# Fewer sum products, last numerators by four heads, and five smaller edits in a four-stage transformer kernel

## The chip, the cores and the metric

The kernel runs on one core of one Trainium2 chip. A core has five engines that run beside each other[...]: PE (TensorE, matrix products), DVE (VectorE), ACT (ScalarE), POOL (GpSimd) and SP (SyncE, which here only issues transfers). Each engine works through its own queue of instructions in order. The metric is the device time of one execution in microseconds (us), the median of several runs.

## The reference, cut to what matters

The input x has four sequences (b) of 512 tokens with 512 features; each sequence has a memory of 1024 rows. Four residual blocks follow each other; each normalises x (layer norm), computes something, and adds it to x, times the tanh of a learned gate.

```python
x = x + tanh(g_xattn[0]) * attention_1_head(layernorm(x), memory, mask)   # stage a
x = x + tanh(g_ffn[0])   * ternary_experts(layernorm(x))                  # stage b
x = x + tanh(g_xattn[1]) * attention_16_heads(layernorm(x), memory)       # stage c
x = x + tanh(g_ffn[1])   * experts_gelu(layernorm(x))                     # stage d

# stage c, for each head (head size 32)
scores = Q @ K.T / sqrt(32)
ctx = softmax(scores) @ V            # numerators exp(score - max), divided by their sum
out = ctx @ Wo.T + bo

# stage d, for expert e, which has tokens 64*e to 64*e+63 of every sequence
h = gelu(xe @ w1[e] + b1[e])
y = h @ w2[e] + b2[e]
```

In stage b the tokens are quantised before the expert's product: a row of a token is scaled, rounded to whole numbers and clipped at 127.

## The kernel before, in words

**Stage a** (to about 300 us) goes through 16 tiles of 128 tokens. Its loop over n runs from -2: `prepare` normalises a tile on DVE, `turn_x` transposes it on PE, `scores` multiplies it with the memory, `softmax` adds a bias that carries the mask (L455) and takes exponentials on ACT, `turn_p` and `readout` make the weighted memory, `finish` adds it to x. Ahead of the loop, ACT takes the tanh of the four gates (L615) and loads the table for logarithm and exponential (L616); then come `prepare(0)`, `set_mask(0)` (the mask's bias, L366, on DVE) and `set_valid(0)` (a reduce over the mask and a product with the gate, L372 and L374). Four weight loads are issued from ACT's queue after the first `turn_x`. Beside the attention the loop prepares stage b: `route_1` to `route_4` normalise, quantise and route the tokens. L531 scales a row and rounds it by adding a large number; L532 takes that number off again, clips, and writes bf16, both on DVE. The same loop makes ternary weights of stage b (`weight_load`, `weight_sum`, `weight_scale`, `weight_store`).

**Stage b** (to about 430 us) runs the ternary experts on sorted tokens. The change does not touch it.

**Stage c** (to about 1284 us) has an order written out by hand: for PE, ACT, DVE and POOL the instructions stand in the order of the program text. The 16 heads of 4 sequences make NG = 16 groups of four heads. A group has U = 16 steps, each one half (two heads, p) of one of the 8 memory chunks (c) of 128 rows. The loop over t runs through all 256 steps. In one turn of it:

- `score_pairs(t)` makes two score tiles for the maxima of step t + 21 (c_s, L1096; DVE takes the row maxima, L1117) and two numerator tiles for step t: a product with ones that puts the negative maximum into the bank (c_t, L1103), the transposed scores on top (L1108), and the exponential on ACT (L1115) into a tile c_e of two heads.
- `add_chunks(t)` sums numerators over chunks, 128x1024 at a time, into four accumulators c_acc: two halves of the chunks (c from 0 to 3, c from 4 to 7) for each pair of heads p. POOL does it, except for the odd steps of the last group, which DVE does two turns later.
- `weigh` multiplies numerators of step t - 4 with the values (c_o, L1147).
- `sum_chunks`, 8 steps after each half of a group, sums an accumulator over its 128 rows with products with ones (c_sum, L1179, four products); for the first half ACT copies the result to c_rec (L1187), for the second DVE adds it (L1189). `divide` then takes reciprocals (L1193) and multiplies (L1196).

All tiles of this stage but c_o come from one ring of 7 PSUM banks (`ps_s`), in the order in which they are asked for: score tiles, numerator tiles, sums, projections and transposes. `project_q`, `project_k`, `project_v` and `project_out` stand at certain steps between. From t = T0 = 236 on no scores are left to make. There the first three sequences are already normalised and transposed for stage d: `normal_d` on DVE (L1216), `turn_d` on PE (d_tp, L1224), `leave_d` on DVE or ACT in turns, one tile a step, twelve in all.

**Stage d** has no hand-written order; a scheduler places its instructions. For each of 8 experts: 16 blocks of the first product (d_h, L1457) with GELU on ACT (L1463), then for two halves of 128 tokens the second product (d_o, L1473, 16 products of 512 columns), to which DVE adds the bias b2 in PSUM (L1477), and then the update of x with the gate for each of the two sequences in the half (L1480). After every second expert a tile of x is complete and is stored (L1487). b2 comes by a load from POOL's queue into one of two buffers (L1450).

Of the kernel before, what the change touches and what calls it, by code (L numbers as in the profile page):

```python
# [18 lines left out]
P = 128  # L19
# [8 lines left out]
def flamingo_kernel(  # L28
# [131 lines left out]
    def ln_stats(b, tag, eng):  # L160

        mv = mv_of.pop(b)
        return mv[:, :, 0], rsqrt(mv[:, :, 1], NT, f"{tag}_{b}", eng)
# [137 lines left out]
    with ExitStack() as st:  # L301
# [61 lines left out]
        def set_mask(p):  # L363
            mk8 = mem_of[p][2]
            bias = wk.tile([P, M], FP, tag="mbias", name=f"mbias_{p}")
            nc.vector.tensor_scalar(bias, mk8, -1.0, -NEG / scale0, ALU.add, ALU.mult)  # L366
            mem_of[p][3] = bias

        def set_valid(p):
# [147 lines left out]
        def route_2(n):  # L517
            xn, am = route_of[n]
            tp = ps_1.tile([P, NK, P], FP, tag="tpx", name=f"b_tp_{n}")
            for k in range(NK):  # L520
                nc.tensor.transpose(tp[:, k, :], xn[:, bass.ts(k, P)], ident)
            xnT = wk.tile([P, NK, P], FP, tag="bxnT", name=f"b_xnT_{n}", bufs=1)
            nc.scalar.copy(xnT, tp)
            amc = sst.tile([P, 1], FP, tag="amc", name=f"b_amc_{n}")
            nc.vector.tensor_scalar(amc, am, Q_EPS, None, ALU.max)  # L525
            ra = sst.tile([P, 1], FP, tag="ra", name=f"b_ra_{n}")
            nc.vector.reciprocal(ra, amc)
            sx = sst.tile([P, 1], FP, tag="sx", name=f"b_sx_{n}")
            nc.vector.tensor_scalar(sx, ra, 127.0, None, ALU.mult)
            row = wk.tile([P, RW], U8, tag="row", name=f"b_row_{n}", bufs=3)  # L530
            nc.vector.tensor_scalar(xn, xn, sx, MAGIC, ALU.mult, ALU.add)  # L531
            nc.vector.tensor_scalar(  # L532
                row[:, 0 : 2 * D].bitcast(BF), xn, -MAGIC, 127.0, ALU.add, ALU.min
            )
            rx = sst.tile([P, 1], FP, tag="rx", name=f"b_rx_{n}")
            nc.gpsimd.tensor_scalar(rx, amc, 1.0 / 127.0, None, ALU.mult)  # L536
            nc.gpsimd.tensor_scalar(
                row[:, 2 * D : RW].bitcast(FP), rx, rx, rx, ALU.mult, ALU.mult
            )
            route_of[n] = xnT, row  # L540
# [71 lines left out]
                weight_sum(q + 2)  # L612

        load_first()
        nc.scalar.activation(gates, graw, AF.Tanh)  # L615
        nc.scalar.preload_act_table_set("natural_log_exp_and_others")  # L616
        prepare(0)
        set_mask(0)
        set_valid(0)
        h = 0  # L620
        for n in range(-2, NQ):
            if 0 <= n < NQ:
                turn_p(n)
            if n >= 0:
                some_weights(h)
                h += 1
            if 0 <= n - 1 < NQ:
                route_1(n - 1)
            if 0 <= n + 1 < NQ:
                scores(n + 1)  # L630
            if n + 2 < NQ:
                turn_x(n + 2)
            if n == -2:
                for q in range(4):
                    weight_load(q, nc.scalar)
            if 0 <= n + 1 < NQ:
                softmax(n + 1)
            if n + 3 < NQ:
                prepare(n + 3)
            if n >= 0 and n % 4 != 3:  # L640
                some_weights(h)
                h += 1
            if n == NQ - 1:
                break
            if 0 <= n - 2 < NQ:
                route_3(n - 2)
            if 0 <= n < NQ:
                finish(n, readout(n))
            if 0 <= n - 1 < NQ:
                route_2(n - 1)  # L650
            if 0 <= n - 2 < NQ:
                route_4(n - 2)
            if n >= -1 and (n + 5) % NT == 0 and n + 5 < NQ:
                load_x((n + 5) // NT)
                load_memT((n + 5) // NT)
                load_mem((n + 5) // NT)
            if n >= 0 and (n + 4) % NT == 0 and n + 4 < NQ:
                set_mask((n + 4) // NT)
            if n >= 0 and (n + 3) % NT == 0 and n + 3 < NQ:
                set_valid((n + 3) // NT)  # L660
# [292 lines left out]
    with ExitStack() as st:  # L953
# [11 lines left out]
        U = 16  # L965
        AHEAD = 21
        LAG = 4

        ones_bf = big.tile([P, P], BF, tag="ones_bf", name="c_ones_bf")
        nc.gpsimd.memset(ones_bf, 1.0)  # L970
# [104 lines left out]
        def score_pairs(t):  # L1075

            todo_t = todo_s = ()
            if t >= 0 and t < NG * U:
                g, k = divmod(t, U)
                c, p = divmod(k, 2)  # L1080
                todo_t = (2 * p, 2 * p + 1)
            u = t + AHEAD
            if u < NG * U:
                gs, ks = divmod(u, U)
# [21 lines left out]
            for i in todo_t:  # L1106
# [2 lines left out]
                    t_of[i], lhsT=kT_of[g][r, bass.ts(c, P)], rhs=qT_of[g][r, :],  # L1109
                    start=False, stop=True,  # L1110
                )
            if todo_t:
                e_of[t] = big.tile([P, 2, S], FP, tag="e", name=f"c_e_{t}", bufs=EB)
            for i in todo_t:
                nc.scalar.activation(e_of[t][:, i % 2, :], t_of[i], AF.Exp)  # L1115
            for i in todo_s:
                nc.vector.tensor_reduce(  # L1117
                    mxn_of[gs][:, j, i, n : n + 1], s_of[i], AX.X, ALU.max
# [41 lines left out]
        def add_chunks(t):  # L1160
# [11 lines left out]
            else:  # L1172
                acc = acc_of[g, c // 4, p]
                eng.tensor_tensor(acc, acc, e_of[t], ALU.add)  # L1174

        def sum_chunks(g, h):
            ps = ps_s.tile([P, S], FP, tag="s", name=f"c_sum_{g}_{h}")
            for i in range(4):
                nc.tensor.matmul(  # L1179
                    ps[i * HD : (i + 1) * HD, :], lhsT=ones[:, 0:HD],  # L1180
                    rhs=acc_of[g, h, i // 2][:, i % 2, :], start=True, stop=True,
                )
            if h == 1 and g == NG - 1:
                return ps
            if h == 0:
                rec_of[g] = wk.tile([P, S], FP, tag="rec", name=f"c_rec_{g}", bufs=1)
                nc.scalar.copy(rec_of[g], ps)  # L1187
            else:
                nc.vector.tensor_tensor(rec_of[g], rec_of[g], ps, ALU.add)  # L1189

        def divide(g, q):
            rq = rec_of[g][:, bass.ts(q, P)]
# [5 lines left out]


        out_of, tp_of = {}, {}  # L1200
        T0 = NG * U - AHEAD + 1

        def reuse_memory():

# [104 lines left out]
        for t in range(-LEAD, NG * U + LAG):  # L1309
# [9 lines left out]
            if (t + LEAD) % U == 0 and 0 <= t + LEAD < NG * U:  # L1319
# [3 lines left out]
                if g >= NK:  # L1323
                    project_k(g, 0)
                    project_k(g, 1)
            d = t - T0
            if 2 <= d < 14:
                leave_d(
                    tp_of.pop(d - 2), *divmod(d - 2, NT), (nc.vector, nc.scalar)[d % 2]
# [1 line left out]
            if 0 <= d < 12:  # L1331
                b, j = divmod(d, NT)
                mean, rstd = stats_of[b]
                xn_of[b, j] = normal_d(b, j, mean[:, j : j + 1], rstd[:, j : j + 1])
            if t >= -AHEAD:
                score_pairs(t)
            if t in early:
                f, args, h = early[t]
# [3 lines left out]
            for b, w, d in [(1, 4, t + LEAD)] + [(b, 8, t + 84 - b * NK * U) for b in (2, 3)]:  # L1342
                if 0 <= d < 4 * w and d % w == 0:
                    back = wk.tile([P, D], FP, tag="xn", name=f"b_back_{b}_{d}")
                    fetch_row(back, b, d // w)
                if 0 <= d < 4 * w and d % w == w // 2 + 1:
                    add_row(b, d // w, nc.gpsimd)
                if w < d < 5 * w and d % w == 1:
                    ln_part(b, d // w - 1, "c")
                if d == 4 * w + 3:  # L1350
                    stats_of[b] = ln_stats(b, "c", nc.gpsimd)
            if 0 <= t < NG * U and not last_odd(t):
                add_chunks(t)
            if last_odd(t - 2):
# [5 lines left out]
            if 0 <= t - LAG < NG * U:  # L1360
                g, k = divmod(t - LAG, U)
                if k == 0 and g % NK == 0 and g:
                    for c in range(NM):
                        project_v(g // NK, c)
                weigh(g, k // 2, k % 2)
            d = t - T0 - 1
            if 0 <= d < 12:
                b, j = divmod(d, NT)
                tp_of[d] = turn_d(ps_s, "s", b, j, xn_of.pop((b, j)), None)
            d = t - 2 * LAG  # L1370
            if 0 <= d < NG * U - 1 and d % 8 == 7:
                sum_chunks(d // U, d % U // 8)

            if (t + LEAD) % (NK * U) == (NK - 1) * U and 0 <= t:
# [43 lines left out]
    with ExitStack() as st:  # L1418
# [13 lines left out]
        for e in range(E):  # L1432
# [33 lines left out]

            r0 = (e * CAP) % P
            j = (e * CAP) // P
            for half in range(B * CAP // P):
                ps = ps_o.tile([P, D], FP, tag="o", name=f"d_o_{e}_{half}")  # L1470
                for f in range(NF):
                    n, fo = divmod(f, NF // NW)
                    nc.tensor.matmul(  # L1473
                        ps, lhsT=hT[:, f, bass.ts(half, P)], rhs=w2c[n][:, fo, :],
                        start=(f == 0), stop=(f == NF - 1),
                    )
                nc.vector.tensor_tensor(ps, ps, b2_t, ALU.add)  # L1477
                for i in range(P // CAP):
                    b = half * (P // CAP) + i
                    nc.vector.scalar_tensor_tensor(  # L1480
                        xs[b][r0 : r0 + CAP, j, :], ps[i * CAP : (i + 1) * CAP, :],
                        gate_f1[r0 : r0 + CAP, :],
                        xs[b][r0 : r0 + CAP, j, :], ALU.mult, ALU.add,
                    )
                    if r0 + CAP == P:
                        eng = nc.sync if e == E - 1 else nc.gpsimd
                        eng.dma_start(out=out[b, bass.ts(j, P), :], in_=xs[b][:, j, :])  # L1487


# [43 lines left out]
```

## Time and profile before

| what | value |
|---|---|
| median of 3 runs | 1734.85 us (1733.16 to 1736.13) |
| the profiled execution itself | 1734.78 us |
| its span, first to last instruction | 1733.0 us |
| mean granted TensorE clock | 0.999 |
| HBM traffic over the span | 99 GB/s |

The rows of the profile name a line of the kernel, an engine, an operation and its tiles as out<-in, with the number of partitions and elements. These carry the places that the change touches (busy time in us, mean of one in ns):

| row | count | busy | mean |
|---|---|---|---|
| DVE L1117, maxima of c_s | 512 | 325.2 | 679 |
| POOL L1174 and L1171, additions to c_acc | 186 | 436.8 | 2374 |
| ACT L1115, exponentials c_e | 512 | 277.9 | 594 |
| PE L1179, c_sum (two passes a product) | 256 | 33.4 | 593 |
| DVE L1193, reciprocals of c_rec | 60 | 56.3 | 941 |
| DVE L1189, additions to c_rec | 15 | 10.3 | 687 |
| DVE L1216, twelve d_xn in stage c | 12 | 17.1 | 1435 |
| DVE L532, whole-number rows | 16 | 6.9 | 428 |
| DVE L1477, additions of b2 | 16 | 11.2 | 700 |

An fp32 product appears on PE as two passes, each with its weight load. Ends of products are modelled, so PE reads as busy even where a product waits for a bank; what a step really takes is seen in the distance from one start of a line to the next.

### The profile page before, as it was taken

The numbers are of one execution on the slowest core, as the hardware profiler recorded it, in microseconds if no ns is written. First come the engines' busy times: TensorE is split into PE (matmuls) and PEld (weight loads), VectorE is DVE, ScalarE is ACT, GpSimd is POOL, SyncE is SP. The second block draws the span as 40 slices with busy tenths as digits, with TensorE's granted clock in tenths as the row PEclk, the third lists the DMA queues.
The fourth block names the chain that finished last, engine by engine and source line by source line (L and its number), as shares of the span: only waits on it lengthen the run. The fifth ranks groups of instructions, "written<-read, shape, count | busy, mean of one in ns | idle before, by whom it ended". The sixth has DMA issues, their size and how long they took to land.

```text
span 1733.0 us, 22272 instructions
## 1 busy us (share of the span) xinstructions
PE 1676.3 (97%) x8805; PEld 826.0 (48%) x8805; DVE 846.4 (49%) x1758; ACT 655.1 (38%) x1155; POOL 635.7 (37%) x594
## 2 busy tenths in 40 slices
PE   5999999888999999999999999999999999999998
PEld 3554555344433434334343343433356776667764
DVE  3888886565577562665626656166850001100111
ACT  3655663485046352353523535235530111011110
POOL 1011111563269494474945748357630000000000
PEclk9999999999999999999999999999999999999999
DMA  9366532595010000010000100001036364534530
GB/s 347 138 245 228 185 128 103 168 325 168 25 50 2 7 13 7 1 50 7 13 7 1 50 1 1 1 1 50 1 120 233 131 220 152 183 139 152 201 121 25
DMA packets 76072, 173.12 MB, mean 100 GB/s; under 512 B 4480, under 2 KB 5008, under 8 KB 75968
## 3 DMA queue, kind: packets, MB, share of 16 engines
q1 hardware_dynamic: 61888, 128.07, 21.0%
q0 software_dynamic: 8368, 33.02, 5.8%
q10 hardware_dynamic: 5712, 10.62, 1.6%
q8 instruction: 69, 1.13, 0.3%
q14 instruction: 35, 0.29, 0.1%
HBM read 153.06 MB, written 18.62 MB: 99 GB/s over the span
## 4 chain that ended last, share of the span: by engine, by line
PE 81%; DVE 9%; POOL 3%; ACT 2%; DMA 2%; issue 2%; DVEq 0%; ACTq 0%; POOLq 0%
PE d_h L1457 13%; PE d_o L1473 13%; PE c_t L1108 9%; PE c_s L1096 8%; PE c_o L1147 8%; PE c_vp L1052 6%; PE c_k L1035 5%; PE c_q L1013 3%; PE a_s L444 3%; PE a_o L479 3%; PE c_out L1065 2%; PE c_t L1103 2%; PE c_sum L1179 2%; DMA b_wt<-tern_d,widx 1%; DVE w_all L412 1%
## 5 line engine op out<-in xcount | busy, mean ns | idle before, releaser
L1117 DVE TENSOR_REDUCE c_mxn<-c_s 128x1 f32<-128x512 f32 x512 | 325.2, 679 | 258.0 <-PE c_s L1096 258.0
L1115 ACT ACTIVATE c_e<-c_t 128x512 f32<-128x512 f32 x512 | 277.9, 594 | 246.2 <-PE c_t L1108 232.9
L1174 POOL TENSOR_TENSOR c_acc<-c_acc,c_e 128x1024 f32<-128x1024 f32 x124 | 291.3, 2378 | 104.7 <-ACT c_e L1115 104.6
L1108 PE MATMUL c_t<-c_qT,c_kT 32*128 32x512 f32 x1024 | 283.7, 595 | 0.0
L1096 PE MATMUL c_s<-c_kT,c_qT 32*128 32x512 f32 x1024 | 276.2, 639 | 0.0
L1473 PE MATMUL d_o<-d_w,d_hT 128*128 128x512 f32 x512 | 221.0, 592 | 0.0
L1457 PE MATMUL d_h<-d_xnT,d_w 128*128 128x256 f32 x992 | 215.4, 379 | 0.0
L1477 DVE TENSOR_TENSOR d_o<-d_o,d_b 128x512 f32<-128x512 f32 x16 | 11.2, 700 | 404.6 <-PE d_o L1473 404.6
L1171 POOL TENSOR_TENSOR c_acc<-c_e,c_e 128x1024 f32<-128x1024 f32 x62 | 145.5, 2367 | 165.8 <-ACT c_e L1115 165.8
L1457 PEld LDWEIGHTS d_h<-d_xnT,d_w 128*128 128x128 f32 x992 | 188.5, 190 | 28.6 <-issue 3.3
L1463 ACT ACTIVATE d_hT<-d_h,b_t 128x256 f32<-128x256 f32 x128 | 60.7, 474 | 350.0 <-PE d_h L1457 350.0
L1147 PE MATMUL c_o<-c_e,c_v 128*32 128x256 f32 x2048 | 162.9, 391 | 0.0
L1473 PEld LDWEIGHTS d_o<-d_w,d_hT 128*128 128x128 f32 x512 | 97.3, 190 | 119.0 <-issue 118.6
L1096 PEld LDWEIGHTS c_s<-c_kT,c_qT 32*128 32x128 f32 x1024 | 74.3, 183 | 116.7 <-issue 41.0
L1147 PEld LDWEIGHTS c_o<-c_e,c_v 128*32 128x32 f32 x2048 | 40.7, 108 | 182.4 <-issue 171.2
L1103 PE MATMUL c_t<-c_mT,c_ones_bf 3*128 3x512 bf16 x512 | 126.9, 380 | 0.0
L444 PE MATMUL a_s<-memT,a_xnT 128*128 128x512 f32 x256 | 117.0, 611 | 0.7 <-ACT a_xnT L436 0.7
L479 PE MATMUL a_o<-mem,a_prT 128*128 128x512 f32 x256 | 114.6, 598 | 0.2 <-ACT a_prT L472 0.2
L1108 PEld LDWEIGHTS c_t<-c_qT,c_kT 32*128 32x128 f32 x1024 | 100.7, 185 | 6.2 <-issue 3.9
L536 POOL TENSOR_SCALAR b_rx<-b_amc 128x1 f32<-128x1 f32 x16 | 3.5, 221 | 244.6 <-DVE b_amc L525 244.6
L1035 PE MATMUL c_k<-c_memT,w_all 128*128 128x512 f32 x192 | 85.3, 597 | 0.0
L1052 PE MATMUL c_vp<-w_all,c_memT 128*128 128x512 f32 x192 | 83.2, 594 | 0.0
(288 smaller groups left out, 1874.5 us busy)
## 6 DMA issues: line engine op xcount, KB each, us to landing
d_w<-in_w SPq DMA_DIRECT2D x63, 1024.0 KB, 5.6
w_all<-in_wuT SPq DMA_DIRECT2D x7, 1024.0 KB, 6.1
w_all<-in_wdT SPq DMA_DIRECT2D x7, 1024.0 KB, 6.0
memT<-in_memT SPq DMA_DIRECT2D x3, 2048.0 KB, 14.6
mem<-in_mem SPq DMA_DIRECT2D x3, 2048.0 KB, 11.2
tern_d<-t ACTq DMA_DIRECT2D x24, 256.0 KB, 4.3
w_all<-in_wgT SPq DMA_DIRECT2D x6, 1024.0 KB, 6.3
c_memT<-in_memT SPq DMA_DIRECT2D x3, 2048.0 KB, 8.1
```

The costliest lines, as they stand in the source:

```text
L444: nc.tensor.matmul(s_ps[:, bass.ts(h, HALF)], lhsT=xnT[:, k, :], rhs=memT_t[:, k, bass.ts(h, HALF)], start=(k == 0), stop=(k == NK - 1),)
L479: nc.tensor.matmul(o_ps, lhsT=prT[:, c, :], rhs=mem_t[:, c, :], start=(c == 0), stop=(c == NM - 1),)
L1035: nc.tensor.matmul(ps, lhsT=wk_t[:, k, bass.ts(o, P)], rhs=memT_of[b][:, k, bass.ts(n, HALF)], start=(k == 0), stop=(k == NK - 1),)
L1052: nc.tensor.matmul(ps, lhsT=memT_of[b][:, k, bass.ts(c, P)], rhs=wv_t[:, k, :], start=(k == 0), stop=(k == NK - 1),)
L1096: nc.tensor.matmul(s_of[i], lhsT=qT_of[gs][r, bass.ts(j, P)], rhs=kT_of[gs][r, bass.ts(n, HALF)], start=True, stop=True,)
L1108: nc.tensor.matmul(t_of[i], lhsT=kT_of[g][r, bass.ts(c, P)], rhs=qT_of[g][r, :], start=False, stop=True,)
L1115: nc.scalar.activation(e_of[t][:, i % 2, :], t_of[i], AF.Exp)
L1117: nc.vector.tensor_reduce(mxn_of[gs][:, j, i, n : n + 1], s_of[i], AX.X, ALU.max)
L1147: nc.tensor.matmul(o_bank[i * HD : (i + 1) * HD, hs], lhsT=v_all[:, c, bass.ts(o * 4 + i, HD)], rhs=e_of[g * U + 2 * c + i // 2][:, i % 2, ...
L1174: eng.tensor_tensor(acc, acc, e_of[t], ALU.add)
L1457: nc.tensor.matmul(ps[:, 0 : B * CAP], lhsT=w1c[n][:, k, bass.ts(fo, P)], rhs=xnT[:, k, :, bass.ts(e, CAP)], start=(k == 0), stop=(k == NK ...
L1473: nc.tensor.matmul(ps, lhsT=hT[:, f, bass.ts(half, P)], rhs=w2c[n][:, fo, :], start=(f == 0), stop=(f == NF - 1),)
```

## The change

1. **Sums of stage c.** For groups 0 to 14 the two accumulator halves are first added by DVE (`join_chunks`, 128x1024, at steps 16g + 18 and 16g + 19, one for each pair of heads), and `sum_chunks` runs once a group, on the joined half. ACT copies the result to c_rec; DVE's addition is gone. The last group keeps its two sums.
2. **Last numerators.** From T0 = 236 on `score_pairs` runs at even steps only and makes the numerators of four heads, those of steps t and t + 1; `weigh` does both halves at even steps.
3. **Turns for stage d** begin at R0 = 223 instead of T0 = 236.
4. **Bias of stage d.** b2 is multiplied by the gate and added to x in SBUF, once an expert (one multiplication of 128x512 and four additions of 64x512), instead of twice into PSUM. Nothing in it depends on the products, and the scheduler puts these instructions of all eight experts ahead of the first update of x; those of the first expert stand between DVE's work on the last tiles of the last sequence.
5. **Last product.** The second half of the last expert is computed in two halves of 256 columns, each with its own updates and stores.
6. **Start.** The tanh of the gates, with a table load on each side of it, moves behind the first tile's root and behind ACT's four weight loads; `set_valid(0)` moves to n = -1, which puts it on DVE between the normalisation of tile 1 and the softmax of tile 0.
7. **To GpSimd:** the mask's bias (`set_mask`) and L532, the whole-number rows.

```diff
         def set_mask(p):
...
-            nc.vector.tensor_scalar(bias, mk8, -1.0, -NEG / scale0, ALU.add, ALU.mult)
+            nc.gpsimd.tensor_scalar(bias, mk8, -1.0, -NEG / scale0, ALU.add, ALU.mult)
...
-            nc.vector.tensor_scalar(
+            nc.gpsimd.tensor_scalar(
                 row[:, 0 : 2 * D].bitcast(BF), xn, -MAGIC, 127.0, ALU.add, ALU.min
             )
...
         load_first()
-        nc.scalar.activation(gates, graw, AF.Tanh)
         nc.scalar.preload_act_table_set("natural_log_exp_and_others")
         prepare(0)
         set_mask(0)
-        set_valid(0)
...
             if n == -2:
                 for q in range(4):
                     weight_load(q, nc.scalar)
+                nc.scalar.activation(gates, graw, AF.Tanh)
+                nc.scalar.preload_act_table_set("natural_log_exp_and_others")
+            if n == -1:
+                set_valid(0)
...
+        T0 = NG * U - AHEAD + 1
...
-                todo_t = (2 * p, 2 * p + 1)
+                todo_t = (2 * p, 2 * p + 1) if t < T0 else range(4)
...
-            if todo_t:
-                e_of[t] = big.tile([P, 2, S], FP, tag="e", name=f"c_e_{t}", bufs=EB)
-            for i in todo_t:
-                nc.scalar.activation(e_of[t][:, i % 2, :], t_of[i], AF.Exp)
+            for m, i in enumerate(todo_t):
+                if m % 2 == 0:
+                    e_of[t + m // 2] = e_t = big.tile(
+                        [P, 2, S], FP, tag="e", name=f"c_e_{t + m // 2}", bufs=EB
+                    )
+                nc.scalar.activation(e_t[:, i % 2, :], t_of[i], AF.Exp)
...
+        def join_chunks(g, p):
+            acc = acc_of[g, 1, p]
+            nc.vector.tensor_tensor(acc, acc, acc_of[g, 0, p], ALU.add)
+
         def sum_chunks(g, h):
...
-            if h == 0:
-                rec_of[g] = wk.tile([P, S], FP, tag="rec", name=f"c_rec_{g}", bufs=1)
-                nc.scalar.copy(rec_of[g], ps)
-            else:
-                nc.vector.tensor_tensor(rec_of[g], rec_of[g], ps, ALU.add)
+            rec_of[g] = wk.tile([P, S], FP, tag="rec", name=f"c_rec_{g}", bufs=1)
+            nc.scalar.copy(rec_of[g], ps)
...
-        T0 = NG * U - AHEAD + 1
+        R0 = NG * U - 33
...
-            d = t - T0
+            d = t - R0
...
-            if t >= -AHEAD:
+            if t >= -AHEAD and (t < T0 or t % 2 == 0):
                 score_pairs(t)
...
+            d = t - U - 2
+            if d >= 0 and d % U < 2 and d // U < NG - 1:
+                join_chunks(d // U, d % U)
             if 0 <= t < NG * U and not last_odd(t):
                 add_chunks(t)
...
-                weigh(g, k // 2, k % 2)
-            d = t - T0 - 1
+                if t < T0:
+                    weigh(g, k // 2, k % 2)
+                elif t % 2 == 0:
+                    weigh(g, k // 2, 0)
+                    weigh(g, k // 2, 1)
+            d = t - R0 - 1
...
-            if 0 <= d < NG * U - 1 and d % 8 == 7:
+            if 0 <= d < NG * U - 1 and d % 8 == 7 and (d % U == 7) == (d // U == NG - 1):
                 sum_chunks(d // U, d % U // 8)
...
+                last = e == E - 1 and half == B * CAP // P - 1
+                for o in ((slice(0, D // 2), slice(D // 2, D)) if last else (slice(0, D),)):
...
-                nc.vector.tensor_tensor(ps, ps, b2_t, ALU.add)
+                    if half == 0:
+                        nc.vector.tensor_scalar(b2_t, b2_t, gate_f1, None, ALU.mult)
+                        for b in range(B):
+                            xt = xs[b][rows, j, :]
+                            nc.vector.tensor_tensor(xt, xt, b2_t[rows, :], ALU.add)
```

## What is predicted, before the changed kernel ran

> **What bounds the kernel now.** I read the page's busy shares, the chain that ended last, and then the timeline of each stage that the change touches.
>
> ```profile
> PE 1676.3 (97%) x8805; PEld 826.0 (48%) x8805; DVE 846.4 (49%) x1758; ACT 655.1 (38%) x1155; POOL 635.7 (37%) x594
> PE 81%; DVE 9%; POOL 3%; ACT 2%; DMA 2%; issue 2%; DVEq 0%; ACTq 0%; POOLq 0%
> ```
>
> PE carries the chain; DVE and POOL are half idle on average. An average hides that in the 16-head stage PE and DVE run in step. Four steps of its timeline (start, duration, engine, line):
>
> ```profile
> 1200.35 0.70 PE L1096 MATMUL c_s<-c_kT,c_qT 32*128 32x512 f32 x2
> 1201.50 1.29 DVE L1117 TENSOR_REDUCE c_mxn<-c_s 128x1 f32<-128x512 f32 x2 [0.47 <-PE c_s L1096]
> 1202.21 0.70 PE L1096 MATMUL c_s<-c_kT,c_qT 32*128 32x512 f32 x2
> 1202.87 2.35 POOL L1171 TENSOR_TENSOR c_acc<-c_e,c_e 128x1024 f32<-128x1024 f32 x1 [0.42 <-ACT c_e L1115]
> 1203.37 1.29 DVE L1117 TENSOR_REDUCE c_mxn<-c_s 128x1 f32<-128x512 f32 x2 [0.58 <-PE c_s L1096]
> ```
>
> A plain step lasts 1.76 or 1.87 us, mean 1.82; DVE's two maxima take 1.29. They begin 1.16 after the step's first product and leave DVE 0.52 free. Seven PSUM banks serve four tiles a step, so the second numerator of step t+1 takes the bank that the first maximum of step t frees. What happens when DVE gets more than 0.52 is seen where reciprocals (L1193, 0.94 each) stand between the maxima: c_s begins at 630.57, 632.33, 634.20, 636.21, 638.20, 640.29, so steps of 1.87 become 2.00 to 2.09. PE's lost time is the delay of the maxima less about 0.13.
>
> The second thing to see is DVE adding while POOL adds:
>
> ```profile
> 1242.06 2.64 POOL L1174 TENSOR_TENSOR c_acc<-c_acc,c_e 128x1024 f32<-128x1024 f32 x1 [2.38 <-ACT c_e L1115]
> 1242.40 3.38 DVE L1171 TENSOR_TENSOR c_acc<-c_e,c_e 128x1024 f32<-128x1024 f32 x1
> 1246.73 2.36 POOL L1174 TENSOR_TENSOR c_acc<-c_acc,c_e 128x1024 f32<-128x1024 f32 x1 [2.03 <-ACT c_e L1115]
> 1249.30 1.21 DVE L1174 TENSOR_TENSOR c_acc<-c_acc,c_e 128x1024 f32<-128x1024 f32 x1
> ```
>
> Alone, DVE's add takes 1.21. Begun while POOL adds, it ends 1.08 after POOL's end (1244.70 to 1245.78). All four such pairs in the trace do so (the others begin at 1258.20, 1261.63 and 1265.13).
>
> **Part 1, sums of the 16-head stage.** Removed: 15 groups of c_sum products, 1.04 us of PE each (steps with one last 2.62 to 2.85 instead of 1.76 or 1.87). DVE's rec add (0.69) goes too, but the steps after it show no delay now, so that is worth 0; ACT's copy moves to an ACT gap (0.7 a step). Added: 30 joins, DVE adds of 128x1024, after the maxima of steps 16g+18 and 16g+19. POOL's first add of the next group overwrites what join 0 reads, so it waits for join 0, and then runs ahead of join 1.
>
> One group, in us from the start of step 16g+18. Maxima end at 2.4; join 0 runs 2.4 to 3.5; POOL's add 3.6 to 5.9; the next maxima 3.5 to 4.7; join 1 waits to 5.9 and ends at 7.0; the maxima of 16g+20 then begin at 7.0, not 3.63 + 1.16 = 4.8. PE loses 2.2 - 0.13 = 2.1. This needs POOL's last add of the old group to be over at 2.4. By the trace it ends at about 0 for groups 4, 8, 12; at 2.0 for 0; at 2.7 for 1, 5, 9, 10, 11; at 4.0 for 2, 3, 6, 7. The last three classes come about 1.0 later, since POOL's queue stays and PE skips the sum before. So: 2.1 x 3; 2.6 for group 0; for the 2.7 class join 0 ends at 4.8, join 1 at 8.3, a loss of 3.3 (group 10); 1, 5, 9 already stall 0.5 there: 2.8 x 3; group 11 hides join 1 behind the value projection (27.7 us of PE): 1.7; in 2 and 6 join 0 ends at 6.1, POOL's row add (1.26) runs beside the maxima and join 1 ends at 8.4: 3.4 x 2; 3 and 7 hide join 1 like group 11, but the maxima behind join 0 begin at 6.0 instead of 2.9: 2.95 x 2. Sum 6.3 + 2.6 + 3.3 + 8.4 + 1.7 + 6.8 + 5.9 = **+35**, against **-13** for the sums of groups 0 to 12 (13 and 14 come below).
>
> [...] By the shortest row (1.2) two joins exceed two gaps by 2 x (1.09 - 0.52) - 0.13 = 1.0 a group: break-even with the sum. [...] Ends for the pair of numbers: 0 and +45.
>
> **Part 2, turns of the last stage begun at step 223.** Steps 223 to 235 last 25.8 now (1193.7 to 1219.5). Twelve d_tp turns (4 transposes, 0.585 of PE each) move in: +7.0; one sum goes: -1.0. DVE gets 12 normalisations (0.55 alone, mean 1.44 now, the rest waiting for POOL) and six copies (0.68) ahead of maxima, in a gap of 1.1 (step 2.4). In some 8 steps POOL is adding: 1.44 + 0.34 - 1.1 = 0.7 each, 5.6; in 3 steps a reciprocal: 0.94 + 0.55 + 0.34 - 1.1 = 0.7 each, 2.1; group 13's joins 2.2. Together **+16**; without waits +7.
>
> **Part 3, numerators by four heads from step 236.** From 1219.5 to the last sum (1270.0) 50.5 us pass now. PE would need 10 pairs of 2.4 (1.82 and a second weigh of 0.57) and two sums, 26. POOL is next: 10 adds of 2.36 after step 236, the rest of one before (2.8), maxima split (1.9), two oT (2.6), two bias adds ahead of the last add (2.4): 33.3, and 7 DVE adds that exclude it, 1.09 each: 41. So **-9.6**. Ends: -20 if POOL overlaps, 0 if the late joins hold the sum product of group 14 for long. Parts 2 and 3 together +6.
>
> **Part 4, the bias of the last experts.** In the built order DVE's first product of b2 with the gate stands before the reciprocal root, d_xn and d_xnT of the last tiles. It waits for b2's load:
>
> ```profile
> 1284.29 1.20 POOL L1450 DMA_DIRECT2D d_b<-in_b  x2 [11.86 <-PE c_out L1254]
> 1286.77 0.54 DVE L1216 TENSOR_SCALAR d_xn<-x,mv_e,rstd_e 128x512 f32<-128x512 f32 x1
> 1287.36 0.66 PE L1224 MATMUL d_tp<-ident,d_xn 128*128 128x128 f32 x4
> ...
> d_b<-in_b POOLq DMA_DIRECT2D x1, 256.0 KB, 7.0
> ```
>
> Issued at 1284.3, 7.0 to land: 1291.3. With 0.55 for the product and 0.87 for root and d_xn the turn begins at 1292.7 instead of 1287.36; the next turn stands behind two 64x512 adds, a copy and d_xn, 2.7 us, of which PE fills 2.1. **+6.0** (4 to 7). The other seven loads come in pairs behind it, within some 40 us; the first expert result is wanted at 1327.9 and two banks cover the rest: 0.
>
> **Part 5, the end.** Now after the last product: b2 add 0.70, two updates 0.75 each, store. The add goes (-0.70), the updates halve (-0.75), the store of half size has about 0.2 less to move: **-1.6**. The halved product pays nothing by the row: L1457's 992 passes of 256 columns take 215.4 us, 0.217 each, half of L1473's 221.0/512 = 0.432, with a 0.19 weight load in each. [...]
>
> **Part 6, the start and the first stage.** The first root waits for the tanh's gates:
>
> ```profile
> 9.60 1.28 ACT L615 ACT_TABLE_LOAD   x1 [9.60 <-DMA graw<-in_g_ffn]
> 12.41 0.29 ACT L280 ACTIVATE lv_a<-mv_a,eps_t 128x1 f32<-128x1 f32 x1
> ...
> 26.06 1.22 DVE L455 CUSTOM_DVE_ANT_0 a_pr<-a_s,mbias 128x1024 f32<-128x1024 f32 x1 [1.60 <-PE a_s L444]
> ```
>
> Its input is there at 6.73, so it comes 5.7 earlier. But ACT now has four weight loads ahead of the tanh, and the fourth is issued 6.6 after the first (15.54, 22.18): then to about 16.9; two table loads, tanh and root bring tile 1 normalised to 21.9, the validity reduce (1.37, now before the softmax) to 23.3 against 26.06: **-2.8** (0 to -5.7). Whole-number rows: DVE sheds 16 x 0.43 and the masks 3 x 0.68; POOL's op of that shape is near its copy (0.60) or its add (1.27), and DVE's next two-input add waits for it: **0** (-5 to +6).
>
> **Sum.** 1734.8 - 2.8 - 13 + 35 + 16 - 9.6 + 6 - 1.6 = 1764.8; taken as 1764. The base is the profiled execution's own 1734.78 (span 1733.0), equal to the median of 1734.85.
>
> **Rivals.** (a) Joins cost DVE's own time alone: part 1 is 0, part 2 some +13: 1740. For it: POOL's adds might fall elsewhere; against: the written dependence puts one between the joins. 15%. (b) The other side: the banks take up DVE's lag, and joins and normalisations stall nothing: -2.8 - 13 + 6.0 - 9.6 + 6 - 1.6 = 1720. It decides if a delay of the maxima under one step is free; the reciprocal steps, lengthened by a delay of 0.3, say no. 9%. (c) Each join loses to one more POOL add in half the groups (2.36 x 13/2) and the first stage pays 6: 1786. 10%. The forecast: 66%. That the change does not do what it says is out: the built order has the 60 products fewer.
>
> **Range and chances.** 1743 to 1780 leaves (b), (c) and half of (a) out. About 0.2%, 3.5 us, is what this kernel's measurement tells from no change. Faster: (b) and a little of (a), 10%. Same: 4%. Slower: 86%.
>
> **What would show it.** Steps 16g+20 and 16g+21 lasting together 2 to 3 us more, DVE's joins near 2 us in the mean, c_sum halved; PE idle 5 us at the second d_tp of the last stage, behind DVE waiting for d_b; the softmax of tile 0 near 23. Joins at 1.2 with steps of 1.9 would break part 1.

## The result and the profile after

The changed kernel takes **1814.68 us** (median of 4 runs, 1812.37 to 1815.5) against 1735.49 for the kernel before in the same session: ratio 1.0453, interval 1.0432 to 1.0473. It is slower, as forecast, but by 79 us where 29 were forecast, and outside the range. Its profiled execution took 1814.32 (span 1812.5).

Three rows of the page after: PE's busy time, the granted TensorE clock in 40 slices, and the chain that ended last.

```profile
PE 1716.9 (95%) x8717; PEld 845.0 (47%) x8717; DVE 923.6 (51%) x1779; ACT 655.2 (36%) x1156; POOL 686.4 (38%) x614
PEclk9999999999998999999899999999989999999999
PE 65%; DVE 7%; POOL 6%; issue 2%; DMA 2%; ACT 1%; DVEq 0%; ACTq 0%; POOLq 0%
```

88 matmuls fewer are recorded, yet PE is busy 41 us longer: the same products took longer. The clock row says how. Before, it is 9 (at least 90%) in every slice; after, three slices show 8. The mean granted clock fell from 0.999 to 0.970. Span times lost clock is 1812.5 x 0.030 = 54 us, against 2 before. DVE and POOL took 13% of the chain instead of 12%; the chain does not name the clock.

The place is seen best at one pair of joins. The timeline of the changed kernel in group 2 (start, duration, engine, line; lines between are left out at ...):

```profile
614.11 9.29 POOL L1179 TENSOR_TENSOR c_acc<-c_acc,c_e 128x1024 f32<-128x1024 f32 x4
...
619.71 1.29 DVE L1122 TENSOR_REDUCE c_mxn<-c_s 128x1 f32<-128x512 f32 x2 [0.58 <-PE c_s L1099]
...
621.12 4.58 DVE L1183 TENSOR_TENSOR c_acc<-c_acc 128x1024 f32<-128x1024 f32 x1
...
623.36 1.25 POOL L248 TENSOR_TENSOR x<-x,b_back 128x512 f32<-128x512 f32 x1
625.62 1.28 DVE L1122 TENSOR_REDUCE c_mxn<-c_s 128x1 f32<-128x512 f32 x2
625.84 2.34 POOL L1176 TENSOR_TENSOR c_acc<-c_e,c_e 128x1024 f32<-128x1024 f32 x1 [1.23 <-DVE c_acc L1183]
626.35 0.58 PE L1106 MATMUL c_t<-c_mT,c_ones_bf 3*128 3x512 bf16 x1 [3.04 <-DVE c_mxn L1122]
...
626.35 2.28 PE L1111 MATMUL c_t<-c_qT,c_kT 32*128 32x512 f32 x4
626.82 2.44 DVE L1183 TENSOR_TENSOR c_acc<-c_acc 128x1024 f32<-128x1024 f32 x1
```

Join 0 (at 621.12) stands behind the last of POOL's four adds (to 623.40) and its row add (to 624.61) and lasts 4.58; a join during which POOL does not add lasts 1.21 to 1.22. The profile shows no wait ahead of it: the two engines meet here in the adds themselves, not by a semaphore alone. The maxima behind it free the bank late, and PE idles for 3.04. This is the mechanism of the forecast. Then the four numerator products take 2.28; in group 0, at whole clock, the same four take 1.23. The windows of this stretch (length, busy time of each engine with the number of its instructions, granted clock PEclk):

```profile
core 0: us, PE busy (x) PEld busy (x) DVE busy (x) ACT busy (x) POOL busy (x), PEclk, DMA share, GB/s
619.45:622.87 3.42, 3.42 (x35) 1.16 (x32) 3.04 (x3) 2.28 (x5) 3.42 (x2) 1.00 0.00 0
622.87:626.28 3.41, 0.44 (x4) 0.00 (x0) 3.41 (x3) 0.36 (x1) 2.18 (x3) 1.00 0.00 0
626.28:629.69 3.41, 3.34 (x16) 1.03 (x16) 3.41 (x4) 1.09 (x2) 2.19 (x2) 0.50 0.00 0
629.69:633.11 3.42, 3.42 (x18) 1.13 (x17) 2.19 (x5) 1.03 (x2) 3.25 (x3) 0.50 0.00 0
```

The window with the stall still has the whole clock. The two windows **behind** it, in which PE is busy again, run at half: 34 matmuls where the window ahead of the stall did 35 in one. So the stall of 3.0 is followed by a loss of another 3.4. All half stretches of the trace last 3.41, 6.83 or 10.24 us, but for the one that the end of the span cuts, and all start on one grid of 3.413 us (from 411.24 to 1366.97 are 280 steps). Ten of the thirteen pairs of joins of groups 0 to 12 have such a stretch behind them, 68.3 us in all.

### The profile page after: what moved, and what is told of

The parts are those of the page before. It is cut to its first block, busy times and chain, and to the rows that moved or that the text cites. A ratio compares the mean times of both kernels' runs of the same rounds, so it can differ in the third digit from the quotient of the medians.

```text
span 1812.5 us, 22176 instructions
## 1 busy us (share of the span) xinstructions
PE 1716.9 (95%) x8717; PEld 845.0 (47%) x8717; DVE 923.6 (51%) x1779; ACT 655.2 (36%) x1156; POOL 686.4 (38%) x614
## 4 chain that ended last, share of the span: by engine, by line
PE 65%; DVE 7%; POOL 6%; issue 2%; DMA 2%; ACT 1%; DVEq 0%; ACTq 0%; POOLq 0%
PE d_o L1489 12%; PE d_h L1470 12%; PE c_t L1111 7%; PE c_s L1099 6%; PE c_vp L1055 6%; PE c_k L1038 5%; PE c_o L1152 5%; PE c_q L1016 3%; DVE c_acc L1183 3%; POOL c_acc L1179 2%; PE c_out L1068 2%; POOL c_acc L1176 2%; DVE c_mxn L1122 2%; DMA b_wt<-tern_d,widx 1%; PE c_t L1106 1%
## 5 line engine op out<-in xcount | busy, mean ns | idle before, releaser
L1111 PE MATMUL c_t<-c_qT,c_kT 32*128 32x512 f32 x1024 | 295.0, 633 | 0.0
L1099 PE MATMUL c_s<-c_kT,c_qT 32*128 32x512 f32 x1024 | 292.0, 671 | 0.0
L1489 PE MATMUL d_o<-d_w,d_hT 128*128 128x512 f32 (+1 forms) x544 | 221.4, 567 | 1.1 <-DVE x L1501 1.1
L1501 DVE SCALAR_TENSOR_TENSOR x<-d_o,gates,x 64x512 f32<-64x512 f32 (+1 forms) x34 | 24.4, 718 | 385.2 <-PE d_o L1489 384.8
L1152 PE MATMUL c_o<-c_e,c_v 128*32 128x256 f32 x2048 | 168.5, 406 | 0.5 <-ACT c_ou L1160 0.5
L1489 PEld LDWEIGHTS d_o<-d_w,d_hT 128*128 128x128 f32 x544 | 103.3, 190 | 114.9 <-issue 109.8
L1106 PE MATMUL c_t<-c_mT,c_ones_bf 3*128 3x512 bf16 x512 | 134.4, 396 | 21.7 <-DVE c_mxn L1122 21.3
L1099 PEld LDWEIGHTS c_s<-c_kT,c_qT 32*128 32x128 f32 x1024 | 78.0, 191 | 113.9 <-issue 52.8
L1507 POOL DMA_DIRECT2D out<-x x12 | 6.5, 542 | 300.5 <-DVE x L1501 300.5
L532 POOL TENSOR_SCALAR b_row<-b_xn 128x512 bf16<-128x512 f32 x16 | 31.0, 1939 | 181.2 <-DVE b_mine L586 161.5
```

What stands on the lines that cost most here:

```text
L1099: nc.tensor.matmul(s_of[i], lhsT=qT_of[gs][r, bass.ts(j, P)], rhs=kT_of[gs][r, bass.ts(n, HALF)], start=True, stop=True,)
L1106: nc.tensor.matmul(t_of[i], lhsT=ones_bf[r, :], rhs=mT_of[g][r, :], start=True, stop=False)
L1111: nc.tensor.matmul(t_of[i], lhsT=kT_of[g][r, bass.ts(c, P)], rhs=qT_of[g][r, :], start=False, stop=True,)
L1152: nc.tensor.matmul(o_bank[i * HD : (i + 1) * HD, hs], lhsT=v_all[:, c, bass.ts(o * 4 + i, HD)], rhs=e_of[g * U + 2 * c + i // 2][:, i % 2, ...
L1489: nc.tensor.matmul(ps[:, o], lhsT=hT[:, f, bass.ts(half, P)], rhs=w2c[n][:, fo, o], start=(f == 0), stop=(f == NF - 1),)
```

## The experiments

Behind each median stand, in brackets, its ratio to the kernel before and the 95% interval of that ratio.

Theory A: a join makes PE stall, and the stall makes the clock fall. Theory B: the clock is beside the point; the losses are longer stalls or come from the other edits.

**e1: the joins taken out.**

```diff
-            d = t - U - 2
-            if d >= 0 and d % U < 2 and d // U < NG - 1:
-                join_chunks(d // U, d % U)
...
+            if h == 0:
                 rec_of[g] = wk.tile([P, S], FP, tag="rec", name=f"c_rec_{g}", bufs=1)
                 nc.scalar.copy(rec_of[g], ps)
+            else:
+                nc.vector.tensor_tensor(rec_of[g], rec_of[g], ps, ALU.add)
```

> The change without its joins: 16 groups sum in two products again, all the rest as changed. Theory A (each join makes the PE stall, and the stall is followed by a stretch of half TensorE clock): groups 0 to 12 give back the 60 us that they lost against before, the joins of groups 13 and 14 some more: about 1750 us, granted clock back to 0.99. Theory B (the joins cost what was worked out, 35 against 13, and the other losses come from elsewhere): 1814.7 - 22 = about 1793.

1749.09 (1.0081, 1.0064 to 1.0097), clock 0.992. In the trace, every step of groups 0 to 12 is as long as before (sum of differences 0.0). So all of the 60 us by which the changed kernel is later at step 223 comes from the joins and the single sums that go with them. Theory A's number holds.

**e10: the joins alone, in the kernel before.** The reverse edit.

> The kernel before with the joins and single sums alone. The changed kernel and the one without joins differ by 65.6 us, so 1735 + 60 to 66: 1795 to 1800. If the joins' cost needed the other edits (the POOL rows or the early turns): under 1780. By the forecast's part 1 alone: 1757.

1806.77 (1.0413, 1.0391 to 1.0436): above A's 1795 to 1800, far above 1757. Groups 0 to 12 lose 60.4, where all edits together lose 60.2; the rest comes behind step 223, where the late joins of groups 13 and 14 are also followed by half clock (17 us of it). The joins need no help from the other edits.

**e2: PE kept busy during the stalls.** What the fills write is overwritten by the numerator that follows.

```diff
+                if i % 2 == 0:
+                    for _ in range(FILL.get(t, 0)):
+                        nc.tensor.matmul(
+                            t_of[i], lhsT=ones_bf, rhs=mT_of[g], start=True, stop=True
+                        )
```

> The changed kernel with 85 useless bf16 matmuls of 512 columns (0.22 us each) put ahead of the first numerator in the steps where the PE stalls behind a join or a normalisation, their number a little under each stall; what they write is overwritten. Theory A (the stall makes the clock fall): the PE stays busy, the clock stays whole, and about 34 us (half of the 68 us of half clock in groups 0 to 12) and 7 more behind step 223 come back, less 2 to 4 for fills that don't fit: about 1777 us, although the PE does 18 us more. Theory B (the loss is the stall itself and the clock does not matter or falls anyway): 1815 to 1822.

The kernel has 99 fills (18 of them ahead of transposes), not the 85 expected, 21 us in all. 1783.53 (1.0278, 1.0261 to 1.0295): 31 us **faster than the changed kernel with 21 us more of matmuls**, clock 0.989. That is 6.5 more than theory A's 1777. Group 0 shows the gain. First the changed kernel, then the filled one: two grid windows each, and from the filled one the three fills.

```profile
527.30:530.71 3.41, 2.68 (x22) 0.86 (x18) 3.41 (x5) 0.91 (x3) 2.18 (x2) 1.00 0.00 0
530.71:534.12 3.41, 3.41 (x26) 0.95 (x18) 1.00 (x3) 1.25 (x3) 3.41 (x3) 0.50 0.00 0
```

```profile
527.97:531.38 3.41, 3.41 (x23) 1.10 (x21) 3.41 (x4) 1.08 (x2) 2.18 (x2) 1.00 0.00 0
531.38:534.79 3.41, 3.41 (x38) 1.30 (x36) 2.26 (x4) 2.12 (x4) 3.41 (x3) 1.00 0.00 0
```

```profile
529.88 0.82 PE L1118 MATMUL c_t<-c_mT,c_ones_bf 128*128 128x512 bf16 x3
```

A visible idle time of 0.73 (3.41 - 2.68) was enough for the clock to fall. It is not all that the window lost: it has 22 matmuls where the one ahead of the stall in group 2 had 35, since PE also reads as busy where a product waits for a bank. With three full-width matmuls in the gap the next window does 38 matmuls instead of 26. Theory B falls. The pairs of joins, loss in us against the kernel before (steps 16g+18 to 16g+29), half clock behind in brackets:

| group | forecast | changed | filled |
|---|---|---|---|
| 0 | 2.6 | 4.1 (3.4) | 2.6 |
| 1, 5, 9 | 2.8 each | 7.0 (10.2), 6.8 (6.8), 6.9 (6.8) | 3.4, 3.4, 3.4 |
| 2, 6 | 3.4 each | 7.2 (6.8), 8.9 (10.2) | 7.3 (3.4), 6.9 (3.4) |
| 3, 7 | 2.95 each | 6.9 (6.8), 5.8 (3.4) | 4.1, 4.1 |
| 4, 8 | 2.1 each | 5.3 (6.8), 5.3 (6.8) | 2.3, 2.3 |
| 10, 11, 12 | 3.3, 1.7, 2.1 | 3.3, 1.7, 2.2 | 3.3, 1.7, 2.2 |
| sum | 35.0 | 71.3 (68.3) | 46.8 (6.8) |

Where the clock stayed whole, the loss is the forecast's within 0.6, but for groups 3 and 7 (1.2 more). In groups 2 and 6 the fills don't fit: 0.72 of idle time stays, the clock falls, and the fills come on top. Taking half of the half-clock time off the changed kernel's losses gives 71.3 - 34.1 = 37.2 for the stalls alone: 35 was forecast.

**e11: the same fills with 3 rows of the array.** `lhsT=ones_bf[r, :], rhs=mT_of[g][r, :]` with the 3 rows of the numerator's own head.

> The filled kernel with the 3 rows of the maxima's products in its fills behind joins instead of 128 rows, and the same 512 columns: the same PE time per fill, hardly any of the array used. If the clock follows the PE's busy share: as the filled kernel, about 1784. If it follows how much of the array works: half clock as in the changed kernel, 1810 to 1820.

1816.19 (1.0474, 1.0458 to 1.049): no help as a whole. It is less clean than meant, since the fills of three ran beside c_s, on other rows of the array, and left the idle time as it was (in group 0 they began at 528.56, c_s at 528.55, and the idle time stayed 0.73); of these places group 0 fell, and groups 4 and 8 kept a whole clock. But groups 5 and 9 fell with PE busy 0.89 and 0.93 of the window. Group 9 of this kernel, and below it two places in the second stage of the changed kernel, where products use 128 rows:

```profile
1033.41:1036.82 3.41, 3.17 (x19) 1.04 (x18) 3.41 (x4) 1.09 (x2) 2.19 (x2) 1.00 0.00 0
1036.82:1040.24 3.42, 3.18 (x15) 1.58 (x14) 2.29 (x6) 0.37 (x1) 3.42 (x2) 0.50 0.00 0
```

```profile
329.32:332.74 3.42, 1.44 (x10) 0.67 (x8) 1.81 (x6) 2.40 (x4) 2.29 (x4) 1.00 0.55 206
332.74:336.15 3.41, 2.35 (x16) 1.23 (x16) 2.16 (x6) 2.11 (x4) 2.32 (x4) 1.00 0.91 261
407.83:411.24 3.41, 1.26 (x8) 0.62 (x8) 2.18 (x8) 1.59 (x3) 0.19 (x1) 1.00 0.20 77
411.24:414.65 3.41, 2.60 (x9) 1.09 (x10) 1.08 (x3) 1.71 (x3) 0.00 (x0) 0.50 0.20 77
```

A window with 3.17 busy of 3.41, mostly of 3- and 32-row products, was followed by half clock; one with 1.44 of 128-row products was not, and one with 1.26 was. PE's busy share alone does not decide.

The kept traces say what fits. Count for each window of the grid how much of the array's work was done: for each product its columns, times the share of the 128 rows and of the 128 columns of the array that it uses, divided by 4096 for fp32 and by 8192 for bf16 and fp8. The two numbers are close to the columns that fit into a window: in the trace before, passes over the whole array start 0.429 us apart for 512 columns of fp32 and 0.215 of fp8, 0.109 and 0.055 for 128 of fp32 and bf16. A window of the last stage, full of 128x128 fp32 products, then comes to 0.98 to 1.00. One pass of c_s, 32*128 with 512 columns, counts 512 x 0.25 / 4096 = 0.03. A step without extras comes to 0.38 in 1.82 us, so a window of such steps to 0.71.

| window, from | PE busy | work | next window |
|---|---|---|---|
| e2, 527.96 (filled) | 1.00 | 0.53 | whole |
| e3, 567.62 | 0.69 | 0.43 | whole |
| e11, 756.93 (group 4) | 0.79 | 0.41 | whole |
| changed, 329.32 (second stage) | 0.42 | 0.39 | whole |
| e8, 1058.27 | 0.77 | 0.38 | whole |
| changed, 755.98 (group 4) | 0.79 | 0.35 | half |
| changed, 527.29 (group 0) | 0.79 | 0.33 | half |
| changed, 407.83 (second stage) | 0.37 | 0.31 | half |
| e11, 1033.40 (group 9) | 0.93 | 0.26 | half |

From 35 us on, the 14 traces have 6878 windows at whole clock; 95 of them are followed by half clock. All 95 have a work of 0.376 or less, and only one of the other 6783 has (0.368). The best cut by PE's busy share misplaces 47. The way back fits too: of 160 windows at half clock, the 65 followed by another have 0.379 or less, the 95 followed by a whole one 0.363 or more. This count was found in the traces afterwards, on modelled ends of products, and no run was built to test it.

**e3 and e8: stalls of a known length in the kernel before.** One or two DVE maxima over a resident tile, behind the maxima of step 16g+22 (e3) or 16g+20 (e8).

```diff
+            for i, n in enumerate(DOSE.get(t, ())):
+                nc.vector.tensor_reduce(lag, xs[0].rearrange(...)[:, 0:n], AX.X, ALU.max)
```

> The kernel before, with one useless maximum over 640 to 2048 columns (0.7 to 2.2 us of DVE, no wait for POOL) behind the maxima of one plain step in each of groups 0 to 11. Stalls alone (the dose less the gap of 0.52 and 0.13): together 9 us, 1744. Theory A: doses of 1280 columns and more stall the PE by 0.7 or more, and each of these seven is followed by 3.4 to 6.8 us of half clock, 1.7 to 3.4 us lost each: 1756 to 1768. Doses of 640 and 896 columns leave the clock whole.

> The kernel before with useless maxima on DVE, as in the first dose, but one step behind the joins' place, where only numerators and weighted values run: at steps 16g+20 of groups 0, 2, 4, 6, 8, 10, 12, of 1280, 1792, 2304, 3072, 1024, 1536, 3840 columns. Stalls alone (dose less 0.65): together 11 us, 1746. Theory A (in these steps a stall of 0.7 lowers the clock): six of the seven are followed by 3.4 to 6.8 us of half clock, 10 to 20 us more: 1756 to 1766. Without half clock in the trace theory A falls.

e3: 1744.09 (1.0054, 1.0037 to 1.0071), clock 0.999: the stalls alone, and theory A's number missed. Three windows had PE busy for 0.69 only and kept the clock: each holds a sum and transposes of 128 rows, and by the count above their work is 0.43 to 0.52. e8: 1756.17 (1.0121, 1.0105 to 1.0136). In its profiled execution the doses of 1024, 1280, 1792 and 2304 columns (1.21, 1.47, 2.01 and 2.6 us of DVE) lost 0.56, 0.83, 1.36 and 1.95 at the third step: each the dose less 0.65, as the forecast's rule has it, with the clock whole (0.1 of it comes back a step later in three of them). (That of 1536, beside delayed maxima already, lost 1.66 of 1.74.) The dose of 3072 (3.4 us) lost 6.2, which is 2.75 by the rule and 3.4 of half clock:

```profile
836.41:839.82 3.41, 0.96 (x7) 0.40 (x4) 3.38 (x6) 0.00 (x0) 3.23 (x3) 1.00 0.08 11
839.82:843.23 3.41, 3.41 (x20) 0.96 (x18) 1.68 (x4) 1.08 (x2) 3.41 (x2) 0.50 0.19 66
```

The dose of 3840 (4.2 us) lost 5.0, with 3.4 of half clock behind it. So two of the six stalls expected to lower the clock did so in this execution, those with a work of 0.10 and 0.26 in their window; the window of the dose of 1536 had 0.38. With no join in it and no wait for POOL, a stall behind DVE still brings half clock. This execution took 1751 at a clock of 0.995, the other three 1755 to 1757 at 0.991 to 0.992: that windows near the edge fall in some executions and not in others is a guess, since only one execution was traced.

**e4: the turns of the last stage begun at step 236 again** (`R0 = T0` in the changed kernel).

> The changed kernel with the turns of the last stage begun at step 236 again, as before the change. If the early turns cost what the trace shows there (19 us between steps 224 and 234) and the stretch behind step 236 has room for them on the PE: about 1796. If the normalisations then exclude POOL's adds in the stretch that POOL bounds (12 of 0.55): 1803. Not under 1790 by either.

1810.77 (1805.21 to 1816.44; 1.0426, 1.0399 to 1.0453): a miss. Steps 223 to 233 lose 4.9 instead of 19.2, but the stretch from 234 to the last sum gains nothing instead of 7.5, and in this execution step 223 came 8 us later than in the changed kernel (2.7 of it ahead of this stage, and 7 us more of half clock among the joins). The four executions at clocks of 0.966 to 0.967 took 1814 and 1816, at 0.971 to 0.974 1805 and 1807. The two parts are one trade: the early turns only move work out of the stretch that four heads shorten.

**e7 and e9: only what was priced as a gain.** No joins, late turns, rows on DVE; tanh behind the loads, four heads, halved last product. e7 adds the bias as before, e9 as changed.

> Only what the sum priced as gains: tanh behind the first loads (-2.8), numerators by four heads from step 236 with the turns as before (-9.6, or -7.5 as the changed kernel's trace shows it), the last product by halves with the bias added as before (-0.9): 1721 to 1724 if these add up; 1730 to 1738 if a stall of the PE in the stretch behind step 236 lowers the clock.

> The same with the changed form of the bias (gate times b2 added to x ahead of the updates). By the changed kernel's trace (4.5 us of idle PE at the second turn of the last stage, half clock behind it, 1.1 at the last product, against 0.4 gained at the end) it is 6 to 7 us slower than the one without it: 1728. If the wait for b2's load were hidden: the same time or 0.4 less.

e7: 1735.74 (1.0002, 0.9993 to 1.0011). No gain. Four heads save what they should on PE and nothing of the time. The windows from 1216 to 1276, summed, of the kernel before and of e7:

```profile
sum 60.00, PE 59.30 PEld 22.60 DVE 44.00 ACT 30.43 POOL 43.04; mean PE 9.88 PEld 3.77 DVE 7.33 ACT 5.07 POOL 7.17
```

```profile
sum 60.00, PE 49.74 PEld 20.20 DVE 44.40 ACT 28.64 POOL 42.46; mean PE 8.29 PEld 3.37 DVE 7.40 ACT 4.77 POOL 7.08
```

PE sheds 9.6, just the forecast's figure, while DVE and POOL keep their 87 of 120. What PE waits for instead, in the timeline of e7:

```profile
1247.01 0.89 PE L1233 MATMUL d_tp<-ident,d_xn 128*128 128x128 f32 x4 [2.50 <-DVE d_xn L1225]
...
1269.03 1.94 PE L1188 MATMUL c_sum<-c_acc,ones 128*32 128x512 f32 x8 [4.12 <-POOL c_acc L1179]
```

The turns wait for normalisations that wait for POOL, the last sum waits for POOL's last add, and the idle windows bring 10 us of half clock (c_sum 1.94 instead of 1.07). From step 234 to the last sum e7 needs 55.7, the kernel before 55.4. How much of that is half clock and how much the waits was not taken apart. e9: 1741.3 (1.0031, 1.0016 to 1.0047), 5.6 more than e7: the new form of the bias.

**e5 and e6: the start.** The tanh's move alone; the whole-number rows and the mask on GpSimd alone.

> The kernel before with only the tanh behind the first weight loads and the validity reduce one step later. The changed kernel's trace has the first softmax 2.77 us earlier. If that lead is kept to the end: 1732. If the second stage gives it back, as it did in the changed kernel (0.1 late when the 16-head stage begins), and the whole-number rows are not the cause: 1735.

> The kernel before with only the whole-number rows and the mask's bias on GpSimd. If these rows (1.94 us each where 0.43 stood) are what gave the start's lead back: 1737 to 1740, with longer idle of the PE at the first transposes of gathered rows (3.3 us instead of 1.6). If they are hidden: 1734.5.

e5: 1734.51 (0.9997, 0.9988 to 1.0006): the first softmax is 2.88 earlier in its trace, the 16-head stage 1.64; what is left at the end can't be told from nothing. Between the two this trace has two half stretches of 3.4 us (at 149.7 and 334.0) that the trace before lacks. e6: 1737.69 (1.0016, 1.0009 to 1.0024): rows and mask cost 2.5 together, and the first transposes of gathered rows wait 3.16 instead of 1.64. The same line before and in the changed kernel (mean ns, then the idle time ahead):

```profile
L532 DVE TENSOR_SCALAR b_row<-b_xn 128x512 bf16<-128x512 f32 x16 | 6.9, 428 | 1.3
```

```profile
L532 POOL TENSOR_SCALAR b_row<-b_xn 128x512 bf16<-128x512 f32 x16 | 31.0, 1939 | 181.2 <-DVE b_mine L586 161.5 <-DVE b_xn L531 19.7
```

**e12: the version that the runs point to.** The kernel before with the tanh's move and the last product by halves in two PSUM banks, the bias as before.

```diff
+                for o in ((slice(0, D // 2), slice(D // 2, D)) if last else (slice(0, D),)):
+                    ps = ps_o.tile([P, D], FP, tag="o", name=f"d_o_{e}_{half}_{o.start}")
```

> The kernel before with the tanh moved and the last product by halves, each half in a PSUM bank of its own and the bias added as before. In the kernels with both halves in one bank the second half's first product waited 1.5 us for DVE's update of the first. If that wait is what ate the end's gain, the end is 1.3 earlier and the start up to 1.6: 1732. If the halves cost for their own (32 more weight loads): 1735.

1732.83 (0.9987, 0.9980 to 0.9993). It beats the kernel before by 0.13%. The last product ends 0.08 later against the turns than before, so the halves cost next to nothing for their own; from its end to the end of the span 4.45 pass instead of 5.7. In one bank (the changed kernel) the second half waits for DVE:

```profile
L1489 PE MATMUL d_o<-d_w,d_hT 128*128 128x256 f32 x64 | 14.2, 381 | 1.1 <-DVE x L1501 1.1
```

## Why the prediction was wrong, step by step

The direction was right and the sum of the stalls too; the step that failed is the rule taken from the reciprocals, "PE's lost time is the delay of the maxima less about 0.13". As a price of the stall alone it holds up to 2.0 us of it (e8). But the stalls that the joins bring leave PE idle for 0.6 to 3.0 us at a time, and behind ten of thirteen pairs of joins the products themselves ran at half clock, 68.3 us in all, which is 34 us lost. The rule put that at nothing: the reciprocals from which it was taken delay the maxima by some 0.3, and no window behind them fell. No term of the sum, and no rival, had the clock in it, because the profile before shows a whole clock in every slice. The lost clock is 52 us more than before, a part of it beside an idle PE; 79.5 - 52 leaves 27, and 29 were forecast.

- **Part 1** (+35 and -13): stalls 37, sums -11 (0.86 each at step 16g+15), half clock +34; together +60. The exclusion of DVE and POOL was read rightly: the mean join lasts 2.44 (1.2 alone, up to 4.58).
- **Parts 2 and 3** (+16 and -9.6): +19.2 and -7.5 in the changed kernel, 13.7 us of half clock among the first; without joins (e1) +13.6 and -9.5. The sum of the two, +11.8 and +4.0, lies on both sides of the forecast's +6.4. But -9.6 was not four heads' own gain: alone they give nothing (e7). PE waits there for POOL and DVE, and its work was counted where its wait should have been.
- **Part 4** (+6.0): right in its wait and its size. d_b's wait and what it holds up, in the changed kernel's timeline:

```profile
1358.00 1.20 POOL L1463 DMA_DIRECT2D d_b<-in_b  x2 [14.42 <-PE c_out L1260]
...
1364.88 0.48 DVE L1495 TENSOR_SCALAR d_b<-d_b,gates 128x512 f32<-128x512 f32 x1 [4.69 <-DMA d_b<-in_b]
1365.54 0.54 DVE L1222 TENSOR_SCALAR d_xn<-x,mv_e,rstd_e 128x512 f32<-128x512 f32 x1
...
1366.13 0.66 PE L1230 MATMUL d_tp<-ident,d_xn 128*128 128x128 f32 x4 [4.48 <-DVE q_e L152]
```

  6.9 from issue to use, 4.5 of idle PE, and half clock behind it; e9 less e7 is 5.6. The idle time is less than the 5.3 forecast, and the half clock, which was not in the sum, made up for it: that the size fits so well is in part luck.
- **Part 5** (-1.6): the end came 1.7 earlier against the last product (the 0.2 of the smaller store was an estimate that no row showed; from the last update's end to the span's end 2.95 passed instead of 3.43), but the halves share a bank, the second waits 1.1, and the last product ended 1.45 later against the first of its stage: 0.3 gained in all. That wait was missed; the weight loads were not the price, as the row had said.
- **Part 6** (-2.8 and 0): the first softmax came 2.77 earlier, as worked out, and the lead was gone before the 16-head stage (0.1 late there). The rows' share is a wrong size: POOL takes 1.94, not 0.60 to 1.27, and rows and mask cost 2.5 instead of 0 (inside the ends given). Which wait of the second stage eats the rest was not tried; one half stretch of 6.8 us lies there.

Rivals (a) and (b) needed joins that POOL's adds don't hold up: 24 of the 30 lasted 1.5 us or more. Rival (c) put more into the stalls; they came to 37 where 35 were forecast, and the excess lies elsewhere.

## What to carry to other kernels

Where products use a small part of the array, as in this stage, a stall of the PE can cost more than its length: here 3.4 to 10.2 us of half clock stood behind ten of thirteen pairs of joins, whose stalls left PE idle for 0.6 to 3.0 us at a time. Price it once as idle time and once with such a stretch behind it, and read the granted clock in windows of 3.4 us, not in slices of 45. Ask how much of the array works in such a window (the falls of these traces stood at 0.376 or less), not how long PE is busy. An engine off the chain that gets an operation which excludes another (DVE's two-input add against GpSimd's: 1.21 alone, 3.38 beside one add in the trace before, up to 4.58 in a join) must be priced by the longest pair in the trace, at the place where the pair will stand. Before counting an engine's saved work as time, ask what that engine waits for in that very stretch.

## What the runs showed of the hardware

The TensorE clock fell to half behind visible idle times far shorter than a window: 0.73 of 3.41 us in the 16-head stage (group 0 of the changed kernel). The longest gap among the joins, 3.04, is shorter than a window too. What separates the windows of these traces is the array's work in them, with a cut near 0.37 of a full window, in both directions (95 falls at 0.376 or less, 95 ways back at 0.363 or more). At half clock, the nine windows of this stage in the changed kernel with PE busy throughout and no product over the whole array come to 0.30 to 0.41, which is about the cut: the way back took one to three windows in the changed kernel, four once in e10. Executions of one kernel spread by 9 to 15 us in e4, e10 and e11, and in e4 the faster ones had the higher clock; the changed kernel spread by 3, those near a whole clock by 2 to 8.

A GpSimd tensor_scalar of 128x512 from fp32 to bf16 took 1.94 us, 4.5 times DVE's 0.43.
